# Where a graph network's exponentials are written: SBUF or PSUM, in layers 1 and 2

## The chip, the cores and the metric

The kernel runs on one core of a Trainium2 chip. The metric is the device time of one execution in microseconds. The engines are TensorE (PE; its weight loads are listed as PEld), VectorE (DVE), ScalarE (ACT), GpSimd (POOL) and SyncE (SP). [...]

## The reference, cut to what matters

Four graph-attention layers work on 4096 nodes of 256 features, with one 4096 x 4096 matrix of neighbours that has some 9 ones to a row, the diagonal among them. Each layer normalises x, keeps the positive part, and adds its attention's output to x.

```
# layer 1
h  = relu(layernorm(x)) @ W.T + b_W
e  = leaky_relu((h @ a1)[:, None] + (h @ a2)[None, :] + b_a, 0.2)
x += softmax(where(adj > 0, e, -9e15), axis=1) @ h

# layer 2
h  = relu(layernorm(x));  g = h @ W
e  = leaky_relu(g @ a[:256] + (g @ a[256:]).T, 0.2)
p  =  softmax(where(adj > 0,  e, -1e12), axis=1) @ h
n  = -softmax(where(adj > 0, -e, -1e12), axis=1) @ h
x += elu(concat([p, n], axis=1) @ wtrans)
```

Layers 0 and 3 have eight and four heads, other scores, and the same mask.

## The kernel before, in words

The kernel uses that the matrix is sparse. The 4096 nodes are cut into NT = 32 tiles of P = 128 rows. A first phase finds the edges, and gives each tile its neighbours in EC = 9 chunks of 128 edges; one more place, SELF, holds the node itself. `nbr[:, t, c]` holds the row numbers of chunk c of tile t.

In each layer a tile goes through the same steps:

1. **Gather** (`gather_early`, `gather_late`, line 909): for each chunk GpSimd issues an indirect DMA that fetches 128 rows of the layer's table from HBM into `g`. GpSimd reads the row numbers from `nbr`, which lies in SBUF. `g` has G = 6 buffers, so the gathers of a tile wait until the tile six before it has been attended. In layers 1 and 3 the chunk LATE is expanded by TensorE from rows kept in SBUF (`expand1`, line 1701) instead of gathered, so these layers have 8 gathers a tile and layers 0 and 2 have 9.
2. **Weights** (`scores` at lines 1777 and 1778, `weigh1`, `weigh2`): VectorE adds the two scores of each edge; ScalarE takes the exponential into `w`, one number per edge (line 1817 in layer 1; lines 1887 and 1888 in layer 2, for both signs); VectorE multiplies the 0/1 matrices `s` (bfloat16, which say to which row each edge belongs) by `w` into `sw` (line 1819 in layer 1; lines 1897 and 1899 in layer 2), and makes the self entry of `sw` (line 1822; lines 1905 and 1906).
3. **Attend** (`attend1`, line 930 by way of `summed`; `attend2`, line 1919): TensorE multiplies `sw` by `g` and sums over the chunks in PSUM.
4. **Finish**: VectorE divides by the sum of weights (lines 1833 and 1929), adds to x, normalises (lines 842 to 845); the row for the next layer's table is made and stored.

Layer 1 has more to do: it makes the 0/1 matrices of a tile from its edge list (`marked`, lines 899 and 903), spreads per-row numbers to the edges (`before1`), and in `give2` TensorE computes at line 1807 the part of layer 2's scores that belongs to the receiving row, into a PSUM tile `pm` that VectorE sums at line 1811. Line 1847 makes layer 2's scores per node, and lines 887 and 888 split them into bfloat16 parts.

The function `run` writes the steps of all tiles down in rounds: each step has a lag, and round r takes step f of tile r - lag. In layer 1 a round holds `give2` of tile r - 3, `weigh1` of r, `finish1` of r - 2, `attend1` of r - 1, `before1` of r + 1, `rows2` of r - 2, `expand1` of r + 1; the gathers are written four rounds ahead. Within an engine instructions may then stand some places from where they were written.

In layer 0 the same weighing is done by `weigh0`, where `w` is a part of a PSUM bank (lines 1534 and 1537). In layers 1 and 2 `w` is a tile of the pool `work` in SBUF, with two buffers. [...] In layer 1 the pools hold: two for `o`, one for `pm`, two for `pe`, three for `s_ps`; in layer 2: four for `o0` and `o1`, three for `pt`.

## Time and profile before

| | |
|---|---|
| median of three runs | 1609.24 us (1608.46 to 1612.63) |
| the profiled execution | 2064.72 us, its span 2062.9 us |
| TensorE's mean granted clock in it | 0.811 of full speed |
| busy in it: PE, DVE, ACT, POOL | 1398.8, 1158.8, 686.5, 1094.1 us |
| gathers of layer 1 in it | from 691.2 to 1095.7 us |
| gathers of layer 2 in it | from 1111.5 to 1550.0 us |

The profile is of one execution, and that one took longer than the runs that were only timed. A row of a group reads: line, engine, operation, what is written and read, shapes, count, then the busy time in us and the mean of one in ns, then the idle time of the engine just before these instructions and what ended it. "issue" is time in which an engine waited for nothing that the profile shows, "remote" a release that the profile can't place. In a timeline each row has its start, its duration, engine, line and operation. In a table of windows each engine has its busy time and, in brackets, its number of instructions.

### The profile page before, as it was taken

What the parts mean: (1) busy time and instruction counts of PE and PEld (TensorE: products, weight loads), DVE (VectorE), ACT (ScalarE), POOL (GpSimd) and SP (SyncE); (2) the same over time, 40 slices, a digit from 0 to 9 for tenths busy, and PEclk for the clock granted to TensorE, in tenths of its full rate; (3) what the DMA queues carried; (4) which work ended last, traced back from release to release, by engine and by line L of the source; (5) the groups of instructions that cost most, each with busy time, mean ns of one, the idle gap of its engine ahead of it and who ended that gap; (6) DMA issues with size and microseconds to landing.
All of it is one profiled execution on the core that took longest, in us unless ns stands there. A gap on an engine that the chain in (4) does not pass through costs nothing.

```text
span 2062.9 us, 24838 instructions
## 1 busy us (share of the span) xinstructions
PE 1398.8 (68%) x7536; PEld 1081.9 (52%) x7536; DVE 1158.8 (56%) x3174; ACT 686.5 (33%) x1798; POOL 1094.1 (53%) x1179
## 2 busy tenths in 40 slices
PE   5735646757666746757577347888889368878886
PEld 3414434534555535646466235666767257656665
DVE  5635745656764435545455224554656258767886
ACT  4645534645342133333332012333334211111110
POOL 2063353544456447657575566566661456656640
PEclk9956767767777867878789677898989679989998
DMA  9875666766344446657576535455553346656630
GB/s 279 296 231 184 198 199 194 254 190 213 97 117 130 120 148 190 184 159 212 155 209 223 167 110 161 145 178 159 167 169 113 112 141 203 216 159 211 193 109 23
DMA packets 169888, 356.67 MB, mean 173 GB/s; under 512 B 32272, under 2 KB 104208, under 8 KB 169744
## 3 DMA queue, kind: packets, MB, share of 16 engines
q0 software_dynamic: 52224, 145.30, 26.2%
q1 hardware_dynamic: 67970, 143.98, 21.2%
q10 hardware_dynamic: 49550, 65.71, 8.9%
q8 instruction: 62, 1.02, 0.2%
q14 instruction: 82, 0.67, 0.1%
HBM read 291.66 MB, written 63.21 MB: 172 GB/s over the span
## 4 chain that ended last, share of the span: by engine, by line
PE 41%; DVE 19%; another core or an unknown queue 17%; issue 12%; ACT 4%; DMA 1%; POOL 0%; DVEq 0%; ACTq 0%; POOLq 0%
PE o L930 20%; PE o L1919 5%; PE pt L1954 3%; PE pt L874 2%; PE pv L2056 2%; PE pv L1701 1%; DVE g L2074 1%; DVE sw L1897 1%; PE pe L1701 1%; DVE s L2061 1%; DVE v L2060 1%; DVE g L1537 1%; PE pt L865 1%; DMA g<-table,nbr 1%
## 5 line engine op out<-in xcount | busy, mean ns | idle before, releaser
L909 POOL DMA_INDIRECT g<-table,nbr x1088 | 1065.6, 979 | 789.0 <-issue 323.0
L930 PE MATMUL o<-g,sw 128*128 128x257 f32 (+1 forms) x1216 | 319.7, 422 | 12.2 <-DVE sw L1822 4.3
L930 PEld LDWEIGHTS o<-g,sw 128*128 128x128 f32 x1216 | 256.2, 213 | 59.9 <-DVE sw L1822 4.7
L1919 PE MATMUL o<-g,sw 128*128 128x257 f32 x896 | 207.3, 390 | 12.1 <-issue 12.1
L1919 PEld LDWEIGHTS o<-g,sw 128*128 128x128 f32 x896 | 177.3, 198 | 40.7 <-issue 12.1
L930 PE MATMUL o<-g,s_f 128*128 128x264 f32 x576 | 169.6, 460 | 0.0
L930 PEld LDWEIGHTS o<-g,s_f 128*128 128x128 f32 x576 | 137.5, 239 | 33.5
L1204 ACT ACTIVATE mask<-adj,minus_half 128x1024 bf16<-128x1024 int32 x112 | 125.1, 1143 | 21.7 <-PE kps L1226 6.4
L1954 PE MATMUL pt<-wt_s,two_t 128*128 128x256 f32 x256 | 93.2, 528 | 57.6 <-ACT two_t L1945 55.3
L2056 PE MATMUL pv<-parts,st 128*128 128x256 bf16 x864 | 110.2, 276 | 30.3 <-issue 26.4
L2060 DVE TENSOR_TENSOR v<-pv,g 128x512 f32<-128x512 f32 (+1 forms) x160 | 94.3, 630 | 45.6 <-remote 40.0
L865 PE MATMUL pt<-ident,r 128*128 128x128 f32 x192 | 45.0, 323 | 104.3 <-issue 33.0
L2056 PEld LDWEIGHTS <-st 128*128 128x128 bf16 x864 | 83.7, 99 | 55.2 <-issue 44.7
L1954 PEld LDWEIGHTS pt<-wt_s,two_t 128*128 128x128 f32 x256 | 65.7, 267 | 81.2 <-ACT two_t L1945 64.5
L2065 ACT ACTIVATE pm<-s 128x40 f32<-128x40 f32 x32 | 6.7, 208 | 293.6 <-DVE s L2063 210.1
L1701 PEld LDWEIGHTS <-st 128*128 128x128 bf16 x768 | 73.4, 99 | 46.4 <-issue 33.2
L2074 DVE SCALAR_TENSOR_TENSOR g<-pm,g 128x2560 f32<-128x2560 f32 x32 | 90.3, 2822 | 12.0 <-issue 10.6
L1537 DVE TENSOR_TENSOR g<-g,pt 128x2560 f32<-128x2560 f32 x32 | 90.0, 2813 | 1.6 <-ACT pt L1534 1.1
L865 PEld LDWEIGHTS pt<-ident,r 128*128 128x128 f32 x192 | 25.9, 161 | 123.6 <-issue 60.2
L930 PE MATMUL o<-g,ident 128*128 128x264 f32 (+1 forms) x128 | 58.4, 547 | 45.0 <-issue 28.0
L1807 PE MATMUL pm<-own,st 128*128 128x3 bf16 x288 | 13.3, 167 | 109.0 <-DVE own L888 56.0
L874 PE MATMUL pt<-wcat,hT 128*128 128x272 f32 (+1 forms) x256 | 75.1, 418 | 14.6 <-ACT hT L867 11.6
(360 smaller groups left out, 2410.8 us busy)
## 6 DMA issues: line engine op xcount, KB each, us to landing
adj<-in_adj_l SPq DMA_DIRECT2D x128, 512.0 KB
ss<-s_of SPq DMA_DIRECT2D x32, 576.0 KB
g<-table,nbr POOLq DMA_INDIRECT x1088
rows_of<-st ACTq DMA_DIRECT2D x16, 832.0 KB
st<-rows_of SPq DMA_DIRECT2D x16, 832.0 KB
x<-x SPq DMA_DIRECT2D x24, 512.0 KB
s_of<-ss ACTq DMA_DIRECT2D x16, 576.0 KB
table<-row ACTq DMA_DIRECT2D x32, 258.0 KB
```

The costliest lines, as they stand in the source:

```text
L865: nc.tensor.transpose(pt[:, k, :], h[:, k * P : (k + 1) * P], ident)
L874: nc.tensor.matmul(pp, lhsT=hT[:, k, :], rhs=w[:, k, :], start=(k == 0), stop=(k == KC - 1))
L909: last = nc.gpsimd.indirect_dma_start(out=g[:, c, :width], out_offset=None, in_=table[: NE if c < EARLY else N, :], in_offset=bass.Indirec ...
L930: nc.tensor.matmul(o, lhsT=a, rhs=b, start=(i == 0), stop=(i == len(pairs) - 1))
L1204: nc.scalar.activation(m, a, AF.Sign, bias=minus_half, scale=1.0)
L1537: nc.vector.tensor_mul(gh, gh, w[:, :, :, None].to_broadcast([P, K, H0, D0]))
L1701: nc.tensor.matmul(ps, lhsT=to[:, b * P : (b + 1) * P], rhs=late_rows[:, b, i, :width], start=(b == 0 and i == 0), stop=(b == LB - 1 and i ...
L1919: nc.tensor.matmul(o, lhsT=sw[:, h, i].rearrange("p s r -> p (s r)"), rhs=g[:, c, : C + 1], start=(i == 0), stop=(i == HC + 1),)
L1954: nc.tensor.matmul(pp, lhsT=lhs[:, k, :], rhs=wt_s[:, k, :], start=(k == 0), stop=(k == 2 * KC - 1))
L2056: nc.tensor.matmul(pv[:, k, :], lhsT=st[:, (a + k) * P : (a + k + 1) * P], rhs=parts[:, i, :], start=(i == 0), stop=(i == 2),)
L2060: nc.vector.tensor_mul(v[:, a : a + n, :], pv[:, :n, :], g[:, a : a + n, :C])
L2074: weighed3[t] = nc.vector.scalar_tensor_tensor(gh, w[:, :, :, None].to_broadcast([P, K, K3, D3]), -math.e, gh, op0=OP.add, op1=OP.mult,)
```

## The change

The exponentials of layers 1 and 2 are written to PSUM in place of SBUF. In layer 1 one bank, `small1`, takes the place of the tiles `pm` and holds both: the result of `give2` in its first 27 columns and `w` at column 64 for even tiles and 96 for odd ones. In layer 2 a bank that was free, `small2`, holds `w` at column 0 or 32. The multiplications read `w` there. Nothing else is edited; after the first added line the line numbers are one higher, in layer 2 two.

```diff
         ) as ps_s:
+            small1 = bank(ps_m, "small1")
...
             def give2(t, of):
                 a, st = a2_of[:, t, :], of.pop("st")
-                pm = bank(ps_m, "pm")[:, : EC * 3].rearrange("p (c s) -> p c s", c=EC)
+                pm = small1[:, : EC * 3].rearrange("p (c s) -> p c s", c=EC)
...
             def weigh1(t, of):
                 s = scores(of["g"], of.pop("a"))
-                w = work.tile([P, EC + 1], F32, name="w")
+                w = small1[:, 64 + 32 * (t % 2) :][:, : EC + 1]
                 nc.scalar.activation(w, s, AF.Exp)
...
-        ) as ps_t:
+        ) as ps_t, tc.tile_pool(name="l2_m", bufs=1, space=PSUM) as ps_m:
+            small2 = bank(ps_m, "small2")
...
             def weigh2(t, of):
                 s = scores(of["g"], a2_of[:, t, :])
-                w = work.tile([P, EC + 1, 2], F32, name="w2")
+                w = small2[:, 32 * (t % 2) :][:, : 2 * (EC + 1)].rearrange("p (c s) -> p c s", s=2)
```

## The prediction

> **What bounds the kernel now.** I first read the page's header and its group of gathers, because a kernel whose GpSimd instructions are almost all of one kind may simply be waiting for them.

> ```profile
> span 2062.9 us, 24838 instructions
> ...
> L909 POOL DMA_INDIRECT g<-table,nbr x1088 | 1065.6, 979 | 789.0 <-issue 323.0
> ```

> Look at three numbers: 1088 gathers, 979 ns each on average, and 323.0 us of "issue", the short pauses between two gathers that nothing explains. The view of line 909 gives both exactly.

> ```profile
> L909 POOL DMA_INDIRECT g<-table,nbr x1088: 940/946/2033, 108.9 to 1997.1; - x182
> ...
>   issue: 323.0, 961
> ```

> The median gather is 946 ns, the longest 2033: some are held up. The pause is 323.0 / 961 = 0.34 us on average and 0.30 in the usual case, so an undisturbed gather costs 0.946 + 0.30 = 1.25 us of GpSimd's time. Layer 1 has 8 gathers a tile (10.0 us) and layer 2 has 9 (11.2 us).

> Next I read the busy time in the two layers' stretches.

> ```profile
> core 0: us, PE busy (x) PEld busy (x) DVE busy (x) ACT busy (x) POOL busy (x), PEclk, DMA share, GB/s
> 752.00:1168.00 416.00, 260.75 (x1612) 209.19 (x1612) 201.29 (x677) 132.54 (x325) 259.88 (x254) 0.79 0.62 188
> 1168.00:1595.00 427.00, 338.24 (x1390) 274.84 (x1390) 213.23 (x601) 137.56 (x577) 253.11 (x257) 0.86 0.51 149
> ```

> Divide by 32 tiles: in layer 1 TensorE works 8.1 us a tile and VectorE 6.3; in layer 2 TensorE works 10.6 and VectorE 6.7. GpSimd with its pauses needs 10.0 and 11.2, before anything holds it up. It is the slowest engine in layer 1 clearly, in layer 2 by a little.

> Yet this execution took 2064.72 us (span 2062.9 and 1.8 around it), 455 us above the median of 1609.24, so its waits can't be taken over as they stand. The timeline of a layer-2 tile shows where it is stretched.

> ```profile
> 1495.44 0.60 PE L1941 MATMUL pt<-ident,two 128*128 128x128 f32 x4
> ...
> 1498.93 0.32 SPq L923 DMA_DIRECT2D g<-table  x1
> 1498.93 0.17 DVE L1929 RECIPROCAL inv<-o 128x1 f32<-128x1 f32 x1 [3.34 <-remote]
> 1498.97 0.37 ACT L867 COPY hT<-pt 128x256 f32<-128x256 f32 x1 [5.91 <-remote]
> ...
> 1499.17 0.95 POOL L909 DMA_INDIRECT g<-table,nbr  x1 [1.93 <-remote]
> ```

> TensorE's last matmul ends at 1496.0; four queues that wait for it all move at 1498.9 to 1499.2. Its completion arrived some 3 us late, and the gathers stood still for it. I choose to read this as an effect of profiling and not of the kernel, for this reason: GpSimd's own work, 1065.6 + 323.0 = 1389 us, leaves only 1609 - 1389 = 220 us of a median run in which it can be idle. Of these, 109 lie ahead of the first gather (it starts at 108.9) and about 65 behind the last (1998.1 to 2062.9), if those ends keep their length. Some 45 us then remain for every other wait of four layers. So in the measured runs **GpSimd's queue of gathers is the bound** through layers 1 and 2.

> **What holds the gathers up.** I put beside each gather the VectorE instruction that was running when it began (from the timeline) and added up what it took over 0.946 us: 36.4 us in all. 27 gathers began under L1819 and lost 15.6 us, 23 under L1897 lost 6.8, 4 under L1899 lost 0.5; all else in the kernel comes to 13.5. One of the first kind:

> ```profile
> 1057.56 1.35 DVE L1819 TENSOR_TENSOR sw<-ss,w 128x1152 f32<-128x1152 bf16 x1
> 1057.70 2.03 POOL L909 DMA_INDIRECT g<-table,nbr  x1 [0.30 <-issue]
> ```

> The gather starts 0.14 us into a multiplication of 1.35 and takes 1.09 us too long; it ends 0.82 after the multiplication does, as if it had read its row numbers only then. Layer 0 has the control: L1537 multiplies the same way, longer, but its weights lie in PSUM.

> ```profile
> 575.45 2.81 DVE L1537 TENSOR_TENSOR g<-g,pt 128x2560 f32<-128x2560 f32 x1
> ...
> 576.17 0.95 POOL L909 DMA_INDIRECT g<-table,nbr  x1 [0.30 <-issue]
> ```

> 33 gathers began under L1537 and lost 0.5 us together.

> [...]

> **The change part by part.**

> Multiplications L1819 (32 x 1350 ns), L1897 (64 x 821) and L1899 (32 x 418): same duration, by the L1537 row. What goes is the hold on the gathers. Lower bound: what the profile shows, 15.6 + 6.8 + 0.5 = 22.9 us. Upper: a gather was held for about the multiplication's remaining time less 0.16 us (mean over the 27 under L1819). If gathers start every 1.25 us without rest, one multiplication of length D costs (D - 0.16)^2 / 2.5: 0.57 us for 1.35, 0.17 for 0.82, 0.03 for 0.42. Times 32, 64 and 32 that is 18.1 + 11.1 + 0.9 = 30 us. I take 16.8 for layer 1 (midway) and 7.3 for layer 2 (as shown, because TensorE's 10.6 us is close behind there): **24 us off the path**.

> Not removed: L1906 (identity by w_s, both SBUF), and L899, L903, L1847 with 5.6 us of held gathers together. They stay as they are.

> L1822 and L1905 read their scalar from PSUM: 64 instructions, [...] on VectorE, which has 3.7 us a tile to spare against GpSimd: nothing on the path.

> The exponentials L1817, L1887, L1888 write to PSUM: the nearest row is L2065, PSUM to PSUM, 208 ns, against 211, 212 and 195 now. Nothing.

> New waits, layer 2: the second exponential waits for the first, in one bank. ScalarE's pair L836 and L837 depends the same way and shows 0.02 us between them (1491.87 + 0.30, then 1492.19). At most 0.1 us x 32 in the chain to sw, which has GpSimd's lead of several tiles over it: nothing.

> New waits, layer 1: small1 holds pm and both w. In the changed program give2's matmuls of tile t wait for the exponential of t + 2, in 7 of 32 tiles for the multiplication L1822 of t + 2 as well. Queued behind on TensorE is attend1 of t + 2, which needs that multiplication anyway; so give2's 0.42 us (nine matmuls of L1807 from 913.65) can slip behind sw at worst. The exponential of t waits for give2 of t - 3, behind which stand sw and all of VectorE's queue; mostly the reduction of pm stands ahead of the scores already, so the wait is old. The orders on TensorE, GpSimd and SyncE are unchanged; those on VectorE and ScalarE shift by a few places in layer 1. Bounds: 0 to 0.42 us x 32 = 13 us, below nothing by no more than a microsecond or two from the reshuffle. As TensorE's 8.1 us stays under 10.0, I take 2.

> Sum: -24 + 2 = -22, on the profiled execution at most 2064.7 - 22 = 2043 (less if its late completions hide it), on the median 1609.2 - 22 = **1587 us**.

> **The rivals.**
> 1. *The next engine takes over.* If the 0.30 us pauses are themselves a product of profiling, the gathers need 1088 x 0.98 = 1066 us, GpSimd has far more slack, and layer 2 goes by TensorE. Then 0 to 8 us come, about 1605. For it: in the profile GpSimd often waits at a tile's start for TensorE. Against it: the 220 us argument, and 961 pauses as regular as a machine cost.
> 2. *The shared bank makes it slower.* exp(t) waits for give2(t - 3), which waits for exp(t - 1): where TensorE is late, VectorE's whole queue stands at sw. It decides from the point at which TensorE's tile in layer 1 passes GpSimd's 10.7 us, that is at 8.1 x 0.79 / 10.7 = 0.60 of full clock over a long stretch. Price 32 x (0.42 for give2 + 0.53 for the reduction and the two steps of scores that then start late: 183 + 174 + 170 ns by their rows) = 30 us, less the 22 gained: 1617. Against it: the mean clock is 0.79 there.
> 3. *The hold remains* because something else than the second SBUF input causes it: 1609. Against it: L1537.
> 4. *More than the profile shows*: uninterrupted gathers meet every multiplication, 30 us: 1579.

> **How the numbers follow.** Chances: forecast 0.60, rival 4 0.12, rival 1 0.13, rival 2 0.11, rival 3 0.04. About 0.3% (4.8 us) is what a measurement here tells from no change. Faster: 0.60 + 0.12 and a quarter of rival 1, 0.75; the same: the rest of rival 1 and rival 3, with 0.01 taken off for noise, 0.13; slower: 0.12. The range leaves out most of rival 2 and the far end of rival 4: 1572 to 1612.

> **What would show it.** In the profile after: the gathers' mean falls from 979 to about 958 ns ((1065.6 - 22.9) / 1088), and hardly any that begins under the multiplications of sw exceeds 1.0 us; these keep 1350, 821 and 418 ns. Wrong if the gathers get shorter and the median doesn't move (rival 1), if ScalarE's w or TensorE's pm shows new waits of over 1 us a tile (rival 2), or if gathers of 1.5 to 2 us remain (rival 3).

## The result, and the profile after

The changed kernel takes 1584.62 us (1577.62 to 1587.77, five runs) against 1609.24 of the kernel before, a ratio of 0.9833 with a 95% interval of 0.9805 to 0.9862. It is faster by some 25 us; the forecast was 22.

The profile that the prediction reads is of a disturbed execution (2064.72 us, granted clock 0.811), so the kernel before was profiled once more as the first experiment; that execution took 1611.41 us. From here on "before" is this second profile. First line 909, the gathers, of before and then after. The columns are the number of gathers and their shortest, median and longest duration in ns; the lines under it give GpSimd's idle time in us and how often.

```profile
L909 POOL DMA_INDIRECT g<-table,nbr x1088: 942/946/2067, 112.7 to 1568.7; - x182
...
  issue: 296.1, 942
```

```profile
L909 POOL DMA_INDIRECT g<-table,nbr x1088: 942/946/1442, 109.4 to 1534.9; - x182
...
  issue: 299.3, 956
```

The median gather is the same; the longest fell from 2067 to 1442 ns. The pauses called "issue" stayed, some 0.31 us each. The mean is in the groups of the two pages, before and then after:

```profile
L909 POOL DMA_INDIRECT g<-table,nbr x1088 | 1077.6, 990 | 373.4 <-issue 296.1
```

```profile
L909 POOL DMA_INDIRECT g<-table,nbr x1088 | 1048.9, 964 | 370.5 <-issue 299.3
```

990 became 964 ns; over all 1088 gathers that is 1077.6 - 1048.9 = 28.7 us of GpSimd's time. Where it fell is plain from one pair of lines each. Both gathers begin 0.14 to 0.15 us into layer 1's multiplication; the first pair is of before, the second of after:

```profile
604.11 1.35 DVE L1819 TENSOR_TENSOR sw<-ss,w 128x1152 f32<-128x1152 bf16 x1
604.26 2.03 POOL L909 DMA_INDIRECT g<-table,nbr  x1 [0.30 <-issue]
```

```profile
628.62 1.35 DVE L1820 TENSOR_TENSOR sw<-ss,small 128x1152 f32<-128x1152 bf16 x1
628.76 0.95 POOL L909 DMA_INDIRECT g<-table,nbr  x1 [0.30 <-issue]
```

The multiplication takes 1.35 us in both; the gather takes 2.03 us under the one and 0.95 under the other. In the whole trace of after, 76 gathers begin under L1820, L1899 or L1901, the three multiplications of sw, and the longest of them takes 0.956 us.

I cut both traces at the first and last gather of each layer, and added up what gathers took over 0.946 us ("held") and GpSimd's pauses above 0.5 us between them:

| gathers of | span before | after | held before | after | long pauses before | after |
|---|---|---|---|---|---|---|
| layer 0 | 402.3 | 399.4 | 10.6 | 9.1 | 40.0 | 38.6 |
| layer 1 | 341.8 | 326.9 | 21.6 | 6.9 | 1.1 | 0.6 |
| layer 2 | 375.5 | 363.0 | 15.9 | 3.4 | 0.0 | 0.0 |
| layer 3 | 320.8 | 320.8 | 1.2 | 1.1 | 0.0 | 0.0 |

Layer 1 lost 14.9 us of its span and 14.7 us of held gathers; layer 2 lost 12.5 and 12.5. What the gathers no longer lose is what the layers no longer take. The 27.4 us of both stand against a difference of 33.8 between the two spans (1609.7 and 1575.9) and of 24.6 between the medians; the after profile is of the fastest of its five runs, and its untouched layer 0 and start are shorter by 2.9 and 3.3 us.

Busy time in the stretch of layers 1 and 2 shows that nothing else became the bound. Before:

```profile
530.30:872.10 341.80, 253.77 (x1676) 213.00 (x1674) 206.60 (x687) 141.90 (x345) 263.96 (x257) 0.87 0.74 229
872.40:1248.00 375.60, 315.55 (x1438) 260.80 (x1438) 222.62 (x638) 141.63 (x591) 288.08 (x288) 0.92 0.64 192
```

After:

```profile
523.80:850.70 326.90, 248.70 (x1666) 209.66 (x1664) 208.51 (x683) 143.90 (x348) 249.28 (x257) 0.88 0.79 239
851.00:1214.10 363.10, 313.50 (x1449) 260.93 (x1447) 220.32 (x640) 143.88 (x591) 275.62 (x288) 0.93 0.67 199
```

The columns after each span are the busy times of TensorE, its weight loads, VectorE, ScalarE and GpSimd, with the number of instructions in brackets; then come TensorE's granted clock, the busy share of the DMA engines and GB/s. Only GpSimd's busy time fell by much, 14.7 and 12.5 us. In layer 2 it is busy 275.6 us and pauses 87.4 us between gathers; the two make up the whole 363.

### The profile page after: what moved, and what is told of

It reads as the page before. It is cut to its first block, busy times and chain, and to the rows that moved or that the text cites. A ratio compares the mean times of both kernels' runs of the same rounds, so it can differ in the third digit from the quotient of the medians.

```text
span 1575.9 us, 24853 instructions
## 1 busy us (share of the span) xinstructions
PE 1269.8 (81%) x7529; PEld 1023.2 (65%) x7536; DVE 1147.5 (73%) x3171; ACT 686.6 (44%) x1801; POOL 1077.8 (68%) x1179
## 4 chain that ended last, share of the span: by engine, by line
PE 34%; DVE 16%; POOL 14%; DMA 11%; issue 9%; ACT 3%; DVEq 0%; ACTq 0%; POOLq 0%; SPq 0%
PE o L930 17%; POOL g L909 13%; DMA g<-table,nbr 11%; PE o L1921 5%; PE pv L2058 3%; DVE g L2076 2%; PE pt L1956 2%; PE pv L1701 2%; DVE sw L1899 1%; PE pt L874 1%; DVE g L1537 1%; PE pt L865 1%; PE pe L1701 1%; DVE s L2063 1%; DVE stats L842 1%
## 5 line engine op out<-in xcount | busy, mean ns | idle before, releaser
L909 POOL DMA_INDIRECT g<-table,nbr x1088 | 1048.9, 964 | 370.5 <-issue 299.3
L930 PE MATMUL o<-g,sw 128*128 128x257 f32 (+1 forms) x1216 | 303.3, 407 | 2.9 <-DVE sw L1823 2.9
L930 PEld LDWEIGHTS o<-g,sw 128*128 128x128 f32 x1216 | 245.5, 204 | 44.5 <-DVE sw L1823 3.3
L1921 PEld LDWEIGHTS o<-g,sw 128*128 128x128 f32 x896 | 173.0, 193 | 51.2 <-issue 24.9
L930 PE MATMUL o<-g,s_f 128*128 128x264 f32 x576 | 152.2, 423 | 0.0
L930 PEld LDWEIGHTS o<-g,s_f 128*128 128x128 f32 x576 | 124.3, 216 | 27.1
L2058 PE MATMUL pv<-parts,st 128*128 128x256 bf16 x864 | 101.1, 275 | 1.3 <-DMA parts<-own 1.3
L2058 PEld LDWEIGHTS <-st 128*128 128x128 bf16 x864 | 85.0, 99 | 12.5 <-DMA parts<-own 1.7
L1537 DVE TENSOR_TENSOR g<-g,pt 128x2560 f32<-128x2560 f32 x32 | 90.0, 2813 | 0.4 <-ACT pt L1534 0.3
L1956 PE MATMUL pt<-wt_s,two_t 128*128 128x256 f32 x256 | 67.9, 411 | 19.7 <-ACT two_t L1947 19.4
L898 ACT ACTIVATE off<-place,minus 128x1152 bf16<-128x1152 f16 x64 | 80.0, 1251 | 7.5 <-DVE st L899 5.8
L2063 DVE TENSOR_REDUCE s<-v 128x36 f32<-128x2304 f32 x32 | 81.7, 2552 | 1.1
L1956 PEld LDWEIGHTS pt<-wt_s,two_t 128*128 128x128 f32 x256 | 49.6, 201 | 34.5 <-ACT two_t L1947 28.0
```

Of the source, the lines that this page charges most:

```text
L909: last = nc.gpsimd.indirect_dma_start(out=g[:, c, :width], out_offset=None, in_=table[: NE if c < EARLY else N, :], in_offset=bass.Indirec ...
L930: nc.tensor.matmul(o, lhsT=a, rhs=b, start=(i == 0), stop=(i == len(pairs) - 1))
L1537: nc.vector.tensor_mul(gh, gh, w[:, :, :, None].to_broadcast([P, K, H0, D0]))
L1921: nc.tensor.matmul(o, lhsT=sw[:, h, i].rearrange("p s r -> p (s r)"), rhs=g[:, c, : C + 1], start=(i == 0), stop=(i == HC + 1),)
L1956: nc.tensor.matmul(pp, lhsT=lhs[:, k, :], rhs=wt_s[:, k, :], start=(k == 0), stop=(k == 2 * KC - 1))
L2058: nc.tensor.matmul(pv[:, k, :], lhsT=st[:, (a + k) * P : (a + k + 1) * P], rhs=parts[:, i, :], start=(i == 0), stop=(i == 2),)
```

## The experiments

### The kernel before, profiled again

> The kernel before, unchanged, profiled once more, to have its stages beside those of the changed kernel (whose profile has a span of 1575.9 us, gathers of layer 1 in 326.9 us and of layer 2 in 363.0 us). Theory (GpSimd's gathers are the bound, and a multiplication with two SBUF inputs holds a gather up until it ends): if this execution is not stretched, the gathers of layer 1 span 327 + 15 to 18 = about 343 us and those of layer 2 363 + 7 to 12 = about 373, with almost no pause above 0.5 us between gathers; layers 0 and 3 are as in the changed kernel within 5 us; gathers begun under L1819, L1897 and L1899 lose 23 to 30 us together. Rival (the next engine, or the instruction order of layer 1, makes the difference): long pauses between gathers in layers 1 and 2, and held gathers well below the difference of the spans.

Nothing is edited. 1611.41 us in its one run, close to the 1612.37 to 1622.80 of sixteen timed runs of this kernel beside it. Layer 1's gathers span 341.8 us and layer 2's 375.5 (expected 343 and 373), pauses above 0.5 us come to 1.1 and 0.0, and layers 0 and 3 stand within 3 us of after. Gathers begun under L1819 lost 16.7 us, under L1897 12.3: together 29.0, near the upper end of the expected 23 to 30. The rival, which wanted long pauses, is out. In the disturbed profile the same layers had 72 and 75 us of them.

### One layer at a time

Layer 1 alone is the changed kernel with

```diff
-        ) as ps_t, tc.tile_pool(name="l2_m", bufs=1, space=PSUM) as ps_m:
-            small2 = bank(ps_m, "small2")
+        ) as ps_t:
...
-                w = small2[:, 32 * (t % 2) :][:, : 2 * (EC + 1)].rearrange("p (c s) -> p c s", s=2)
+                w = work.tile([P, EC + 1, 2], F32, name="w2")
```

> Layer 1's weights in PSUM, layer 2's in SBUF as before. Theory (held gathers): 15 to 18 us below the kernel before, about 1592, and the gathers of layer 2 are held up again for 7 to 12 us. Rival (it is layer 1's shifted order on VectorE and ScalarE that pays): the whole 25 us, 1584. Rival (the shared bank costs, layer 2 pays): above 1600.

Layer 2 alone is the changed kernel with

```diff
-            small1 = bank(ps_m, "small1")
...
-                pm = small1[:, : EC * 3].rearrange("p (c s) -> p c s", c=EC)
+                pm = bank(ps_m, "pm")[:, : EC * 3].rearrange("p (c s) -> p c s", c=EC)
...
-                w = small1[:, 64 + 32 * (t % 2) :][:, : EC + 1]
+                w = work.tile([P, EC + 1], F32, name="w")
```

> Layer 2's weights in PSUM, layer 1 as before, its instruction order too. Theory (held gathers): 7 to 12 us below the kernel before, about 1600, and with the run of layer 1 alone the two gains add up to the whole of about 25. Rival (layer 1's order): within 3 us of the kernel before. Rival (TensorE bounds layer 2, so freed gathers wait there): within 3 us of the kernel before, with pauses above 0.5 us between layer 2's gathers.

| | median us | ratio to before | span of layer 1's gathers | of layer 2's | held in 1 | held in 2 |
|---|---|---|---|---|---|---|
| layer 1 alone | 1592.81 | 0.9844 (0.9819 to 0.9868) | 326.3 | 372.5 | 6.4 | 12.8 |
| layer 2 alone | 1606.13 | 0.9929 (0.9905 to 0.9952) | 345.8 | 364.7 | 25.6 | 4.9 |

The kernel before had a median of 1615.99 beside these. Each half frees its own layer's gathers and leaves the other's held: against the profile of before, layer 1's span is 15.5 us shorter in the one and layer 2's 10.8 in the other, together 26.3 against 27.4 for both at once. So layer 2 is not bound by TensorE, and layer 1's shifted order isn't what pays: layer 2 gained without it, and with layer 1's order alone layer 2's gathers are still held by 12.8 us.

The measured times fit less well. Layer 1 alone came out 23.2 us below the kernel before (1.6%), where 15 to 18 were expected, and can't be told by its time from the whole change (0.9833); layer 2 alone came out 9.9 us below (0.7%), inside the expected 7 to 12. The two should have added up to about 25 and give 33, with each ratio uncertain by a quarter of a per cent, 4 us, to either side; the profiled run of before, 1611.41, lies 4.6 us under the median of the runs beside it. So the time of layer 1 alone would not rule out that its change brings everything; the time of layer 2 alone does, and so do the held gathers of both. For the sizes I rest on the spans.

### Layer 0 the other way

```diff
-            w = b[:, 128 : 128 + K * H0].rearrange("p (k h) -> p k h", h=H0)
+            w = work.tile([P, K, H0], F32, name="w0")
```

> The changed kernel, with layer 0's weights w moved the other way, from PSUM to SBUF, so that L1537's multiplication (2560 elements, 2813 ns) gets two SBUF inputs. Theory (hold): L1537 keeps its 2.81 us; the first gather that begins under each is held until it ends, 2.81 - 0.16 - 0.62 = 2.0 us on average x 32 = 64 us of held gathers in place of 0.3; layer 0 has 38.6 us of pauses above 0.5 us that can take some of it up, so the time rises by 30 to 64 us over the changed kernel, to 1615 to 1650. Rival (where the operand lies doesn't matter to the gathers): within 5 us of the changed kernel.

1622.31 us, a ratio to before of 1.0040 (1.0023 to 1.0058): 2.1% above the changed kernel's 0.9833, some 33 us, near the lower end of the expected 30 to 64. The first line is from the groups of VectorE, the others from the timeline.

```profile
L1537 DVE TENSOR_TENSOR g<-g,w 128x2560 f32<-128x2560 f32 x32 | 90.2, 2818 | 0.5 <-ACT w L1534 0.5
```

```profile
445.56 2.81 DVE L1537 TENSOR_TENSOR g<-g,w 128x2560 f32<-128x2560 f32 x1
446.76 2.43 POOL L909 DMA_INDIRECT g<-table,nbr  x1 [0.30 <-issue]
...
459.78 2.81 DVE L1537 TENSOR_TENSOR g<-g,w 128x2560 f32<-128x2560 f32 x1
460.28 3.14 POOL L909 DMA_INDIRECT g<-table,nbr  x1 [0.30 <-issue]
```

L1537 keeps its 2.82 us, and the gathers under it take 2.43 and 3.14. The 28 that began under it lost 55.3 us (expected about 64), and layer 0's held time rose from 9.1 to 62.1. Its long pauses shrank from 38.6 to 28.8, so 53.0 - 9.8 = 43.2 us should show, and its span grew by 43.4 (399.4 to 442.8). That this is more than 33 is in part the choice of executions: the changed kernel's profile is 7 us below the median of its runs, this one 5 us above. The hold comes back with the operand's place alone, and only what the pauses can't swallow reaches the time.

### The hold by itself, and VectorE's time by itself

Both are the changed kernel with a further multiplication per tile in layer 1, whose result is used nowhere; they differ in its second input.

```diff
-                    sw[:, :EC, :], of.pop("s"), w[:, :EC, None].to_broadcast([P, EC, P])
+                    sw[:, :EC, :], of["s"], w[:, :EC, None].to_broadcast([P, EC, P])
...
+                more = only.tile([P, EC, P], F32, name="more", bufs=1)
+                nc.vector.tensor_mul(
+                    more, of.pop("s"), ident_b[:, None, :].to_broadcast([P, EC, P])
+                )
```

> The changed kernel with one more multiplication per tile in layer 1 (its result is used nowhere): the 0/1 matrices by ident_b, 1152 elements, both inputs in SBUF, 32 x 1350 ns = 43 us of added VectorE work. Theory (hold): layer 1's gathers lose 16 to 19 us more than in the changed kernel (6.9 us there), their span rises from 327 to about 344, and the time by 14 to 20 us, although VectorE has 3.7 us a tile to spare. Rival (a gather is held by any VectorE work, or VectorE is the bound): the same rise as in the run whose added multiplication reads PSUM.

The other has w, in PSUM and in float32, in place of `ident_b`, which is bfloat16.

```diff
-                    sw[:, :EC, :], of.pop("s"), w[:, :EC, None].to_broadcast([P, EC, P])
+                    sw[:, :EC, :], of["s"], w[:, :EC, None].to_broadcast([P, EC, P])
...
+                more = only.tile([P, EC, P], F32, name="more", bufs=1)
+                nc.vector.tensor_mul(
+                    more, of.pop("s"), w[:, :EC, None].to_broadcast([P, EC, P])
+                )
```

> The same added multiplication per tile in layer 1, same length, but its second input is w in PSUM. Theory (hold): no gather is held by it, layer 1's gathers span 327 within 3 us, and the time is that of the changed kernel within 5 us, for 43 us of added VectorE work. Rival (VectorE is the bound, or the shared bank's waits cost): 14 us or more above the changed kernel.

The tile `more` in the two, SBUF first: count, then shortest, median and longest duration.

```profile
L1827 DVE TENSOR_TENSOR more<-ss,ident_b x32: 1342/1351/1382, 572.2 to 878.7; 128x1152 f32<-128x1152 bf16 x32
```

```profile
L1827 DVE TENSOR_TENSOR more<-ss,small x32: 1340/1347/1353, 571.2 to 861.2; 128x1152 f32<-128x1152 bf16 x32
```

The same 43 us of VectorE's time were added. With SBUF the median was 1601.6 us (0.9930, 0.9904 to 0.9955), with PSUM 1580.12 (0.9806, 0.9780 to 0.9831), both beside a before of 1612.77: 21.5 us between them. Against the changed kernel's 0.9833 the first is about 1.0% slower, some 16 us (expected 14 to 20), and the second can't be told from it, as expected. With SBUF 32 gathers began under the added multiplication and lost 20.5 us, and layer 1's gathers span 345.5 us; with PSUM they span 326.8, as in the changed kernel (326.9). VectorE's time costs nothing here; its second SBUF input does. The two second inputs differ in type as well as in place; in the run on layer 0 only the place changed.

### Two more operands moved

```diff
-    def marked(pool, t, st):
+    def marked(pool, t, st, late_in=None):
...
-        off = pool.tile([P, (EC - EARLY) * P], BF16, name="off_late", bufs=1)
+        off = late_in
+        if off is None:
+            off = pool.tile([P, (EC - EARLY) * P], BF16, name="off_late", bufs=1)
...
-                    marked(first, t, of[t]["st"])
+                    marked(first, t, of[t]["st"], small1[:, 192 : 192 + (EC - EARLY) * P])
...
-                w_s = small.tile([P, 2], F32, name="w_s")
+                w_s = small2[:, 64 + 32 * (t % 2) :][:, :2]
```

> The changed kernel with two more operands moved to PSUM: w_s in layer 2 (in small2), and layer 1's off_late (as float32 in small1), so that L1906's and layer 1's L903's operations have one SBUF input each. Theory (hold): held gathers fall by 1 to 3 us of the 20 left in the changed kernel, the time by as much, which the runs can hardly tell from none. Rival (small1 now ties the marking of tiles four rounds ahead to the weighing, so GpSimd comes to wait): pauses above 0.5 us appear in layer 1 and the time rises by 5 us or more.

`off_late`, which line 903 reads in layer 1, and `w_s`, which makes layer 2's self entry, move to PSUM. 1579.75 us, 0.9793 (0.9768 to 0.9818). Held time fell by 0.6 us each in layers 1 (6.9 to 6.3) and 2 (3.4 to 2.8), together 1.2 of the expected 1 to 3, and no long pause appeared in either. It is the lowest ratio of the study, but the run with the added PSUM multiplication, 0.9806 beside it, can't be told from it. Inconclusive as an improvement; as a hint on what is left, clear: little.

## Why the prediction was right, point by point

**GpSimd's gathers as the bound: right, and the argument held.** The budget of 220 us was made of the time ahead of the first gather (109.4 us; taken as 109), the time behind the last (40.1; taken as 65) and other waits (taken as 45). The profile after shows 39.2 us of long pauses between gathers of a layer and 16.3 between layers, 55.5 in all. Rival 1's premise, that profiling makes the pauses of 0.30 us, falls: they fill layer 2 together with the gathers, and yet this profiled execution took 1577.62 us, no longer than the other four of its kernel, which were only timed (1582.94 to 1587.77).

**The stretched profile: right not to take its waits over, wrong about the cause.** I put TensorE's late completions down to profiling. But the eight other profiled executions took what timed runs take. It was that one execution, with a granted clock of 0.811 where the second profile has 0.891; what disturbed it stays open.

**The hold: shown.** Moving the operand removes it (layers 1 and 2), brings it back (layer 0), and it can be added with VectorE's time kept the same (the added multiplications). In the eight undisturbed profiles together, 115 gathers begin well inside a multiplication of sw that reads w in SBUF (0.1 us or more after its start, 0.2 or more before its end, with nothing else running on VectorE just then): each takes over 1.0 us, up to 2.14. Of 364 that begin so under a multiplication with w in PSUM, one takes over 1.0 us, 1.04. When the prediction was made, the second SBUF input as the cause was my estimate, from the contrast of L1819 with L1537; the run on layer 0, with 55.3 us lost under L1537, bears it out. That it is the reading of the row numbers that is held up in a gather was not tested; the runs show that the gather is.

**Layer 1's term was right in size, its parts by luck.** 16.8 taken, less 2 for new waits, 14.8 forecast; 14.9 measured. Gathers under L1819 lost 16.7 us before and those under L1820 none after, but those under other instructions lost 2 us more after. That happens to be the size that I had set aside for waits, which is another thing. Nor is the agreement to 0.1 us more than luck: in the run with layer 2 alone, layer 1 is as before and its gathers span 345.8 us, not 341.8. Measured from there the gain is 18.9, so a layer's gain is known to some 4 us from one pair of profiles.

**Layer 2's term was too small.** I took the lower bound, 7.3, as TensorE's 10.6 us a tile seemed close behind. The measured 12.5 is a little more even than the upper bound (11.1 + 0.9), and L1897 alone held 12.3 us where the bound has 11.1; measured from the run with layer 1 alone, where layer 2 is as before and spans 372.5 us, the gain is 9.5. The lower bound came from a profile with 74.6 us of long pauses between layer 2's gathers, in which 23 of them began under L1897, against 32 in the undisturbed one; that the pauses are why is likely, but not shown. And TensorE had more room than I gave it: its busy time in layer 2 is 313.5 / 32 = 9.8 us a tile.

**New waits: none on the path.** The tile `small` after, with its waits (us, times):

```profile
L1818 ACT ACTIVATE small<-s x32: 159/182/183, 566.2 to 854.9; 128x10 f32<-128x10 f32 x32
...
  DVE s L1778: 129.3, 53
  DVE own L888: 57.7, 14
  DVE a_of L1812: 19.5, 4
  ACT small L1890: 14.7, 32
```

The tile `w` before, and then `pm` before:

```profile
L1817 ACT ACTIVATE w<-s x32: 195/212/213, 572.6 to 875.7; 128x10 f32<-128x10 f32 x32
...
  ACT w L1888: 11.0, 30
```

```profile
L1807 PE MATMUL pm<-own,st x288: 164/166/188, 594.3 to 887.7; 128*128 128x3 bf16 x144
...
  DVE own L888: 66.3, 18
```

`give2` waited for L888 before and does now (66.3, then 57.7 us); behind that the new waits hardly show: 1.5 us, once, for the multiplication L1823. A wait of the exponential for the reduction of pm (L1812) shows more: 19.2 of the 19.5 us above, in three times, which is more than I allowed for. But it takes the place of other waits: all that ScalarE stood idle before layer 1's exponentials fell from 118.3 to 95.1 us. And it is hidden, since GpSimd has only 0.6 us of long pauses in layer 1: the gathers are written four rounds ahead. Layer 2's second exponential now starts 0.03 us after the first ends, where it had started 0.09 us ahead of that end (medians of the 25 tiles in which the two stand next to each other, before in its first profile). VectorE's wait for it grew from 11.0 to 14.7 us, 0.12 us a tile where 0.1 was the bound, also hidden.

**Durations.** The multiplications kept theirs (1352 and 1347, 820 and 818, 418 and 415 ns). L1537, by whose row this was foreseen, takes 2814 ns with w in PSUM (after) and 2818 with it in SBUF (the run on layer 0). Of the two instructions that now read their scalar from PSUM, L1822's mean rose from 338 ns (first profile of before) to 398 and L1905's fell from 222 to 214: 1.9 us more and 0.3 less in all. The forecast mean of a gather, 958, was 979 less the stalls; against the undisturbed 990 the fall was 26 where 21 was foreseen.

**Rival 4**, 30 us, was nearer for layer 2 than the forecast. **Rival 2** never came to its point of decision: TensorE's tile in layer 1 is 248.7 / 32 = 7.8 us, under the gathers' 326.9 / 32 = 10.2. That this tile grows as the clock falls, on which its 0.60 rests, was my estimate and is not shown.

## What to carry to other kernels

Where GpSimd's indirect gathers pace a stage, count what VectorE reads while they start, not only how long VectorE works. Here a multiplication of 1.35 us with two SBUF inputs held the gather that began under it (2.03 us), and moving the small one of the two to PSUM freed the gather (0.95 us) at no cost in the multiplication (1352 and 1347 ns). To size such a gain, compare each instruction's longest duration with its median, list what ran on the other engine when the long ones began, and look for a place in the same kernel where the operand already lies elsewhere. And before waits of a profile are used, hold its length against the timed runs.
